# Block kernel on one core: maxima sent from SyncE, the attention division on GpSimd, and a reordered closing part

## The chip, the cores and the metric

The kernel runs on 1 core of one Trainium2 chip. The metric is the device time of one execution in microseconds, the median of several runs. The core has TensorE (PE, matmuls and transposes), VectorE (DVE), ScalarE (ACT), GpSimd (POOL) and SyncE (SP, which here issues DMAs only). ACT also issues some DMAs; while it issues one, it starts no computation.

## The reference

A pre-norm transformer block on 16 sequences of 256 tokens, width 256, all in float32. Attention has 16 heads of width 16; a key more than 16 places ahead of the query is masked. The feed-forward part has 1024 units and weights that are interpolated from control points.

```python
scores = jnp.einsum('bihd,bjhd->bhij', q, k) * scale
mask = idx[None, :] - idx[:, None] > WINDOW // 2
scores = jnp.where(mask[None, None, :, :], -jnp.inf, scores)
attn = jax.nn.softmax(scores, axis=-1)
out = jnp.einsum('bhij,bjhd->bihd', attn, v).reshape(b, s, d)
...
x = x + _L0_attn_ref(_layernorm(x, axis=-1), wq, wk, wv, wo)
x = x + _L0_ffn_ref(_layernorm(x, axis=-1), gate_cp, up_cp, down_cp)
# _L0_ffn_ref: (silu(h @ gate_w.T) * (h @ up_w.T)) @ down_w.T
```

## The kernel before

Every engine runs its instructions in the order in which the program lists them (`InOrder`), so the order of the calls is the schedule. The main loop goes over steps s = 0 to 16 and works on several sequences at once: `nb = s-1` is having its score maxima found, `tb = s-2` its exponentials taken, `ob = s-3` its attention divided and projected, `gb = s-4` its gate and up products made, and `db = s-5` its down sums. The projections for sequence s+3 are spread over the step in places called gaps (`project(s, gap)`). From step 13 on (`LATE`) there is no such sequence, so these steps have less TensorE work. After step 16 a closing part, written out by hand, finishes the last sequences; `last` is 15.

A step has six score visits: `inner(nb, tb, g)` for the groups g = 0 to 3 and `outer(nb, tb, 0)` and `(…, 1)`, in the order inner 0, inner 1, outer 0, inner 2, inner 3, outer 1. A visit writes raw scores for `nb` and scores less their maxima for `tb` into two PSUM tiles (`tiles`, named scores in the profile). Then `read` empties them: ACT takes exponentials (`e`) of one tile while DVE finds maxima (`z`, `mx`) in the other, and then they change over; POOL masks the exponentials (affine selects). The next visit's matmuls wait until both tiles have been read. What TensorE does in between are fillers: `project`, `down` sums (eight units for each half of a sequence, two recorded matmuls a unit), `gate_up`, `values`, `project_o`, and transposes.

The maxima reach the scores by way of a row of the key tile: `turn_max` transposes the maxima of half the groups (pm), ACT copies them (mxT), and two DMAs that ACT issues write them into row 31 of `qks`. Half 0 serves the visits inner 0, inner 1 and outer 0 of the next step, half 1 the other three. In the loop before, `turn_max(nb, 1)` is the last thing in a step.

The sums of the exponentials make a round trip through DRAM. `gather` sends them (den) and the heads' outputs (ac) from `au` on SP at the end of a step. In the next step `invert` takes the reciprocal on DVE in the middle of inner 0 (after it for s < 4), and SP then issues, in this order: two DMAs of feed-forward inputs (`feed`), `send_inverse` (rd), two more of `feed`, and `spread_inverse`, four DMAs (rb) that wait for rd to land. `divide` multiplies ac by rb, and `project_o` (py) needs the product. `stats_f`, `norm_f`, `turn_f` and `features` make the feed-forward input from it. All results of `project_o`, `values`, `turn_max`, `turn_f`, `features` and most `down` sums share two PSUM buffers (`ps_m`).

In the closing part the order before is: inner 0 and 1 together, four SP items as above, `down(12, 0)`, outer 0, `divide(14)`, half a down sum, `gate_up(13, 0)`, `project_o(14)`, `values(15, 0)`, then inner 2 and 3, outer 1, and the feed-forward part of sequences 13 to 15. No maxima are left to be found there, so DVE has no part in its visits.

Of the kernel before, what the change touches and what calls it, by code (L numbers as in the profile page):

```python
# [141 lines left out]
def block_kernel(  # L142
# [354 lines left out]
    def inner(nb, tb, *groups, between=None):  # L497

        has_n, has_t = 0 <= nb < B, 0 <= tb < B
        qn, qt = qks[nb % NQK], qks[tb % NQK]  # L500
        places = [(g, S * gi, S * gi if len(groups) > 1 else S) for gi, g in enumerate(groups)]
        for g, at_t, at_n in places:
            if has_n:
                if g == 0:
                    mxs[nb] = sb.tile([P, 2, H], F32, tag="mx", name=f"mx{nb}")
                scores(qn, True, g, P, at_n, P + HB + LOOK)
            if has_t:
                scores(qt, False, g, HB, at_t + HB - LOOK, S - HB + LOOK)
            if has_n:
                scores(qn, True, g, P + HB, at_n, S)  # L510
            if has_t:
                scores(qt, False, g, 0, at_t, S)

        def exponentials(pr):
            for g, at, _ in places:
                e = sb8.tile([P, 2, S], F32, tag="e0", name=f"e0{tb}_{g}_{pr}")
                act.activation(e, tiles[pr][:, :, at : at + S], AF.Exp, scale=HD**-0.5)

                pool.affine_select(
                    out=e[:, :, 0:M0], in_=e[:, :, 0:M0],  # L520
                    compare_op=ALU.is_ge, fill=0.0, base=LOOK,
                    pattern=[[0, 2], [1, M0]], channel_multiplier=-1,
                )
# [44 lines left out]
    def turn_max(b, half):  # L568
        mx = mxs[b] if half == 0 else mxs.pop(b)
        pm = ps_m.tile([H // 2, S], F32, tag="m", name=f"pm{b}_{half}")  # L570
        for c in range(2):
            pe.transpose(
                pm[:, c * P : (c + 1) * P], mx[:, c, H // 2 * half : H // 2 * (half + 1)], ident
            )
        mxT = sb.tile([H // 2, S], F32, tag="mxT", name=f"mxT{b}_{half}")
        act.copy(mxT, pm)
        for i in range(2):
            act.dma_start(qks[b % NQK][31:P:32, 0, 2 * half + i, :], mxT[4 * i : 4 * i + 4, :])


    def values(b, g2):
# [32 lines left out]
    def invert(b):  # L614
        den = recs.pop(b)
        rec = sb.tile([4 * H, 64], F32, tag="rec", name=f"rec{b}")
        dve.reciprocal(rec, den)
        recs[b] = rec
# [45 lines left out]
                )  # L664
        recs[b] = pr

    def divide(b):
        dve.tensor_tensor(aos[b], aos[b], recs.pop(b), ALU.mult)


    def project_o(b):
        py = ps_m.tile([P, 2, DIM], F32, tag="m", name=f"py{b}")
        ao = aos.pop(b)
        for c in range(2):
            for kc in range(2):
                pe.matmul(
                    py[:, c, :],
                    lhsT=ao[:, kc, c * P : (c + 1) * P],
                    rhs=w_in["o"][:, kc, :],
                    start=(kc == 0),  # L680
                    stop=(kc == 1),
                )
        dve.tensor_tensor(xs[b], xs[b], py, ALU.add)

    def stats_f(b):
        norm_stats(b, "f")
# [91 lines left out]
    def do(stage, b, *args):  # L778
        if 0 <= b < B:
            stage(b, *args)  # L780
# [56 lines left out]
    def project(s, gap):  # L837
        for stage, *what in early.get((s, gap), ()):
            stage(*what)
        pb = s + AHEAD  # L840
        for stage, b, at, *what in (
            (stats_a, pb + 1, 1),
            (scale_xT, pb, 1),
            (first_part, pb, "a"),
            (send_factors, pb + 1, "b"),
            (second_part, pb, 4),
            (load_xT, pb + 1, 4),
            (spread, pb, 4),
            (spread_factors, pb + 1, 5),
            (project_v, pb, 6),  # L850
        ):
            if at == gap and b >= RAW:
                do(stage, b, *what)
# [10 lines left out]
    for s in range(B + 1):  # L864
        nb, tb, ob, gb, db = s - 1, s - 2, s - 3, s - 4, s - 5
        late = s >= LATE

        if s < 4:
            inner(nb, tb, 0)
            project(s, 1)  # L870
            do(invert, ob)
        else:
            inner(nb, tb, 0, between=(lambda: invert(ob)) if ob < B else None)
        do(feed, ob - 1, (0,))
        do(send_inverse, ob)
        do(feed, ob - 1, (1,))
        do(spread_inverse, ob)
        if s >= 4:
            project(s, 1)
        do(down, db, 0, ALL[0:4] if late else ALL[0:6], ALL, fb[:, 0, 0:DIM])  # L880
        inner(nb, tb, 1)
        if late:
            down(db, 0, ALL[4:8])
        else:
            do(down, db, 0, ALL[6:8])
            do(down, db, 1, ALL[0:4])
        project(s, 2)
        outer(nb, tb, 0)
        do(divide, ob)
        project(s, 3)  # L890
        if late:
            down(db, 1, ALL[0:3], ALL[0:4])
        else:
            do(down, db, 1, ALL[4:8])
            do(send_out, db)
        do(gate_up, gb, 0)
        project(s, "a")
        if late:
            down(db, 1, ALL[3:4], ALL[0:4])
        do(project_o, ob)  # L900
        project(s, "b")
        inner(nb, tb, 2)
        if s <= 1:
            project(s, 4)
        do(stats_f, ob)
        if s > 1:
            project(s, 4)
        if late:
            do(turn_max, nb, 0)
            down(db, 1, ALL[4:6], ALL[4:6], fb[:, 1, 0:DIM])  # L910
        inner(nb, tb, 3)
        do(norm_f, ob)
        project(s, 5)
        if not late:
            do(turn_max, nb, 0)
        do(values, tb, 0)
# [24 lines left out]
    down(last - 3, 0, ALL)  # L941
    outer(-1, last, 0)
    divide(last - 1)
    down(last - 3, 1, FIRST, FIRST)
    gate_up(last - 2, 0)
    project_o(last - 1)
    values(last, 0)
    stats_f(last - 1)
    inner(-1, last, 2, 3)
    norm_f(last - 1)  # L950
    down(last - 3, 1, SECOND, SECOND)
    send_out(last - 3)
    turn_f(last - 1)
    send_samples(last - 1)
    outer(-1, last, 1)
    down(last - 2, 0, FIRST, FIRST)
    gate_up(last - 2, 1)
    values(last, 1)
    aos[last] = sb1.tile([P, 2, S], F32, tag="ac", name=f"ac{last}")
    invert_last(last)  # L960
    features(last - 1)
    feed(last - 1)
    invert_rows(last)
    down(last - 2, 0, SECOND, SECOND, tiles[0][:, 1, 0:DIM])
    down(last - 2, 1, ALL[0:2], ALL, tiles[0][:, 0, 0:DIM])
    spread_last(last)
    divide(last)
    down(last - 2, 1, ALL[2:4])
    project_o(last)
    stats_f(last)  # L970
    norm_f(last)
    down(last - 2, 1, ALL[4:8])
    send_out(last - 2)
    gate_up(last - 1, 0)
# [5 lines left out]
    down(last - 1, 0, FIRST + SECOND, FIRST + SECOND)  # L980
    gate_up(last, 0)
    down(last - 1, 1, FIRST, FIRST)
    gate_up(last, 1, (tiles[0], tiles[1]))
    down(last - 1, 1, SECOND, SECOND)
    send_out(last - 1)
    order = FIRST + SECOND
    halves = [fb[:, n, 0:P] for n in range(2)]
# [53 lines left out]
```

## Time and profile before

| | |
|---|---|
| three runs | 537.41, 531.87, 530.50 us; median 531.87 |
| the profiled execution's own time | 533.38 us |
| its span, first to last instruction | 531.3 us |
| busy: PE / DVE / ACT / POOL | 492.3 / 354.1 / 230.9 / 154.7 us |
| PE busy, 150 to 350 us | 197 of 200 us |
| PE busy, 375 to 450 us | 66.7 of 75 us |
| PE busy, 475 us to the end | 47.2 of 56.3 us |
| granted TensorE clock, mean | 0.99 |

The profile is one execution. A line of the timeline gives an instruction's start, its length, its engine and what it writes and reads; "idle before" is time in which the engine did nothing, with what ended it. "q" behind an engine's name means its sequencer, which issues DMAs. PE records of matmuls overlap, so the start of the next group tells more than the length of one. Steps 5 to 12 start 29 us after one another, steps 13 to 16 27.2 us.

### The profile page before, as it was taken

What the parts mean: (1) busy time and instruction counts of PE and PEld (TensorE: products, weight loads), DVE (VectorE), ACT (ScalarE), POOL (GpSimd) and SP (SyncE); (2) the same over time, 40 slices, a digit from 0 to 9 for tenths busy, and PEclk for the clock granted to TensorE, in tenths of its full rate; (3) what the DMA queues carried; (4) which work ended last, traced back from release to release, by engine and by line L of the source; (5) the groups of instructions that cost most, each with busy time, mean ns of one, the idle gap of its engine ahead of it and who ended that gap; (6) DMA issues with size and microseconds to landing.
All of it is one profiled execution on the core that took longest, in us unless ns stands there. A gap on an engine that the chain in (4) does not pass through costs nothing. (4 is left out here: it accounts for less than half of the span.)

```text
span 531.3 us, 18475 instructions
## 1 busy us (share of the span) xinstructions
PE 492.3 (93%) x7491; PEld 349.9 (66%) x7491; DVE 354.1 (67%) x1468; ACT 230.9 (43%) x434; POOL 154.7 (29%) x282
## 2 busy tenths in 40 slices
PE   8998969899999999999999999999898989899987
PEld 7666655457767677776777776766565656566656
DVE  4786356576777667676867677676878686835463
ACT  1236343545363635445454636354444444453130
POOL 6338541222323232323223232322222221222000
PEclk9999998989999999999999999999999999998999
DMA  3541833315243434434252423323040404041231
GB/s 118 145 97 41 259 90 92 110 35 155 64 131 102 111 104 113 124 83 143 61 155 72 133 81 94 122 62 106 15 132 3 144 4 147 3 144 40 81 101 41
DMA packets 53241, 51.26 MB, mean 96 GB/s; under 512 B 6354, under 2 KB 52100, under 8 KB 53156
## 3 DMA queue, kind: packets, MB, share of 16 engines
q1 hardware_dynamic: 46772, 44.24, 28.6%
q10 hardware_dynamic: 6384, 5.84, 3.6%
q8 instruction: 59, 0.97, 0.8%
q14 instruction: 26, 0.21, 0.1%
HBM read 24.12 MB, written 12.84 MB: 70 GB/s over the span
## 5 line engine op out<-in xcount | busy, mean ns | idle before, releaser
L136 DVE CUSTOM_DVE_ANT_0 z<-scores,mask 128x144 bf16<-128x144 f32 (+1 forms) x512 | 156.4, 362 | 85.4 <-issue 38.5
L136 ACT ACTIVATE e<-scores 128x512 f32<-128x512 f32 (+1 forms) x192 | 114.9, 615 | 140.0 <-PE scores L136 74.4
L136 POOL TENSOR_SCALAR_AFFINE_SELECT e<-e 128x224 f32<-128x224 f32 (+1 forms) x192 | 92.4, 487 | 278.3 <-ACT e L136 275.7
L136 PE MATMUL scores<-qk 31*64 31x208 f32 (+7 forms) x4096 | 105.7, 318 | 19.7 <-ACT e L136 11.1
L136 PEld LDWEIGHTS scores<-qk 32*64 32x64 f32 (+1 forms) x4096 | 70.2, 131 | 52.2 <-ACT e L136 36.8
L136 PE MATMUL pd<-downT,inter 128*128 128x256 f32 x216 | 53.8, 390 | 0.5 <-DVE inter L136 0.5
L136 PE MATMUL po<-e,v 128*32 128x256 f32 (+1 forms) x1024 | 51.4, 339 | 1.4 <-POOL e L136 0.9
L136 PEld LDWEIGHTS po<-e,v 128*32 128x32 f32 x1024 | 30.1, 111 | 23.9 <-issue 9.5
L136 DVE SCALAR_TENSOR_TENSOR th<-th,scores 128x512 f32<-128x512 f32 x34 | 23.4, 687 | 33.6 <-ACT th L136 33.6
L136 PEld LDWEIGHTS pd<-downT,inter 128*128 128x128 f32 x216 | 39.2, 189 | 9.7 <-issue 2.5
L136 DVE DVE_READ_ACCUMULATOR2_ANT mx<- 128x1 f32 x512 | 42.5, 83 | 0.0
L136 PE MATMUL fb<-downT,inter 128*128 128x256 f32 x168 | 41.9, 391 | 0.0
L136 PE MATMUL fb<-feat,gate_w 32*64 32x256 f32 x480 | 40.5, 395 | 0.8 <-DMA feat<-via 0.7
L136 ACT ACTIVATE th<-scores 128x512 f32<-128x512 f32 x34 | 20.1, 597 | 45.3 <-PE scores L136 45.3
L136 PE MATMUL scores<-feat,gate_w 32*64 32x256 f32 x544 | 36.7, 394 | 1.3 <-ACT e L136 1.2
L136 PEld LDWEIGHTS fb<-downT,inter 128*128 128x128 f32 x168 | 30.1, 189 | 11.0 <-DVE inter L136 3.9
L136 PE MATMUL py<-wo,ac 128*128 128x256 f32 x128 | 31.7, 392 | 5.0 <-issue 2.6
L136 ACT COPY au<-po 128x512 f32<-128x512 f32 x32 | 18.7, 586 | 30.6 <-PE po L136 15.5
L136 PE MATMUL pk<-xT,wk 128*128 128x256 f32 x128 | 31.7, 390 | 0.0
L136 PE MATMUL pq<-xT,wq 128*128 128x256 f32 x120 | 30.4, 397 | 0.5 <-ACT xT L136 0.5
L136 PEld LDWEIGHTS py<-wo,ac 128*128 128x128 f32 x128 | 24.5, 194 | 9.5 <-issue 3.2
L136 PE MATMUL pv<-wv,xT 128*128 128x256 f32 x120 | 30.0, 390 | 0.0
(94 smaller groups left out, 615.4 us busy)
## 6 DMA issues: line engine op xcount, KB each, us to landing
qk<-qkc SPq DMA_DIRECT2D x31, 256.0 KB
feat<-via SPq DMA_DIRECT2D x62, 128.0 KB
x<-x SPq DMA_DIRECT2D x16, 256.0 KB
ac<-au SPq DMA_DIRECT2D x32, 128.0 KB
via<-x2T SPq DMA_DIRECT2D x16, 256.0 KB
via<-x2T ACTq DMA_DIRECT2D x16, 256.0 KB
rb<-rd SPq DMA_DIRECT2D x60, 64.0 KB
out<-x SPq DMA_DIRECT2D x15, 256.0 KB
```

Source lines behind the costliest of these rows:

```text
L136: return self.tc.keep_in_program_order(fn(*args, **kwargs))
```

## The change

- `turn_max` no longer sends. A new `send_max` does it. From step 4 on SP issues the sends: half 0 in the second half of the step, half 1 in the following step behind `spread_inverse`. For s < 4 ACT still does it. In steps 13 to 16 `turn_max` of half 1 also moves into the following step, behind inner 0.
- `divide` runs on POOL from step 4 to 16 and is listed ahead of outer 0 (before: on DVE, behind it). In step 3 it stays on DVE, but behind inner 2, with `project_o` and `stats_f` behind inner 3 and `norm_f` behind outer 1.
- The addition of `project_o`'s result becomes a call of its own, `add_o`; in steps 13 to 16 it is behind inner 2.
- In steps 13 to 16 the eight units of `down(db, 0)` stand as 4, 3 and 1 (the last behind outer 0) in place of 4 and 4, and in the shared PSUM buffers.
- The closing part has all its visits first, with only `down(12, …)` between them, and the rest in a new order behind them.

```diff
@@ turn_max
         act.copy(mxT, pm)
+        mxTs[b, half] = mxT
+
+    mxTs = {}
+
+    def send_max(b, half, queue=sp):
+        mxT = mxTs.pop((b, half))
         for i in range(2):
-            act.dma_start(qks[b % NQK][31:P:32, 0, 2 * half + i, :], mxT[4 * i : 4 * i + 4, :])
+            queue.dma_start(qks[b % NQK][31:P:32, 0, 2 * half + i, :], mxT[4 * i : 4 * i + 4, :])
...
-    def divide(b):
-        dve.tensor_tensor(aos[b], aos[b], recs.pop(b), ALU.mult)
+    def divide(b, engine=dve):
+        engine.tensor_tensor(aos[b], aos[b], recs.pop(b), ALU.mult)
...
-        dve.tensor_tensor(xs[b], xs[b], py, ALU.add)
+        pys[b] = py
+
+    pys = {}
+
+    def add_o(b):
+        dve.tensor_tensor(xs[b], xs[b], pys.pop(b), ALU.add)
@@ main loop
-            inner(nb, tb, 0, between=(lambda: invert(ob)) if ob < B else None)
+            inner(nb, tb, 0, between=lambda: invert(ob))
+        if late:
+            turn_max(tb, 1)
         do(feed, ob - 1, (0,))
         do(send_inverse, ob)
         do(feed, ob - 1, (1,))
         do(spread_inverse, ob)
-        if s >= 4:
+        if s > 4:
+            send_max(tb, 1)
+        if not first:
             project(s, 1)
-        do(down, db, 0, ALL[0:4] if late else ALL[0:6], ALL, fb[:, 0, 0:DIM])
+        if late:
+            down(db, 0, ALL[0:4])
+        else:
+            do(down, db, 0, ALL[0:6], ALL, fb[:, 0, 0:DIM])
         inner(nb, tb, 1)
         if late:
-            down(db, 0, ALL[4:8])
+            down(db, 0, ALL[4:7])
...
         project(s, 2)
+        if not first:
+            divide(ob, pool)
         outer(nb, tb, 0)
-        do(divide, ob)
         project(s, 3)
         if late:
+            down(db, 0, ALL[7:8])
             down(db, 1, ALL[0:3], ALL[0:4])
...
-        do(project_o, ob)
+        if not first:
+            project_o(ob)
+        if not (first or late):
+            add_o(ob)
         project(s, "b")
         inner(nb, tb, 2)
         if s <= 1:
             project(s, 4)
-        do(stats_f, ob)
+        if first:
+            do(divide, ob)
+        elif late:
+            add_o(ob)
+        if not first:
+            stats_f(ob)
         if s > 1:
             project(s, 4)
         if late:
-            do(turn_max, nb, 0)
+            turn_max(nb, 0)
+            send_max(nb, 0)
             down(db, 1, ALL[4:6], ALL[4:6], fb[:, 1, 0:DIM])
         inner(nb, tb, 3)
-        do(norm_f, ob)
+        if first:
+            do(project_o, ob)
+            do(add_o, ob)
+            do(stats_f, ob)
+        else:
+            norm_f(ob)
         project(s, 5)
         if not late:
             do(turn_max, nb, 0)
+            if first:
+                do(send_max, nb, 0, act)
         do(values, tb, 0)
         if s:
             do(load_x, s + 2 + AHEAD)
+        if not (first or late):
+            send_max(nb, 0)
         outer(nb, tb, 1)
+        if first:
+            do(norm_f, ob)
         project(s, 6)
...
-        do(turn_max, nb, 1)
+        if s + 1 < LATE:
+            do(turn_max, nb, 1)
+        if first:
+            do(send_max, nb, 1, act)
         project(s, 7)
@@ closing part, the new order whole
     inner(-1, last, 0, 1)
+    turn_max(last, 1)
     invert(last - 1)
     feed(last - 2, (0,))
     send_inverse(last - 1)
     feed(last - 2, (1,))
     spread_inverse(last - 1)
+    send_max(last, 1)
+    down(last - 3, 0, ALL[0:5])
     outer(-1, last, 0)
+    down(last - 3, 0, ALL[5:8])
+    inner(-1, last, 2, 3)
+    down(last - 3, 1, ALL)
+    send_out(last - 3)
+    outer(-1, last, 1)
     divide(last - 1)
+    values(last, 0)
     gate_up(last - 2, 0)
+    values(last, 1)
+    aos[last] = qks[(last - 1) % NQK][:, 0, 0:2, :]
+    invert_last(last)
     project_o(last - 1)
+    add_o(last - 1)
     stats_f(last - 1)
+    gate_up(last - 2, 1, (tiles[0], tiles[1]))
+    invert_rows(last)
+    down(last - 2, 0, FIRST, FIRST + SECOND, fb[:, 0, 0:DIM])
+    spread_last(last)
     norm_f(last - 1)
+    divide(last)
+    down(last - 2, 1, FIRST[0:2], FIRST + SECOND, fb[:, 1, 0:DIM])
     turn_f(last - 1)
     send_samples(last - 1)
+    project_o(last)
     features(last - 1)
     feed(last - 1)
+    add_o(last)
     stats_f(last)
     norm_f(last)
+    down(last - 2, 1, FIRST[2:4], FIRST + SECOND)
+    down(last - 2, 0, SECOND, FIRST + SECOND)
+    down(last - 2, 1, SECOND, FIRST + SECOND)
     send_out(last - 2)
     turn_f(last)
     send_samples(last)
+    gate_up(last - 1, 0)
     features(last)
     gate_up(last - 1, 1, (tiles[0], tiles[1]))
     feed(last, (0, 1), sp, act)
+    down(last - 1, 0, FIRST, FIRST + SECOND)
+    down(last - 1, 1, FIRST, FIRST + SECOND)
     gate_up(last, 0)
+    down(last - 1, 0, SECOND, FIRST + SECOND)
     gate_up(last, 1, (tiles[0], tiles[1]))
+    down(last - 1, 1, SECOND, FIRST + SECOND)
     send_out(last - 1)
```

More of the change, by code (lines that the diff above doesn't have):

```diff
@@ L866, in block_kernel @@
         late = s >= LATE
-        if s < 4:
+        first = s < 4
+        if first:
             inner(nb, tb, 0)
@@ L929, in block_kernel @@
         do(features, ob)
-        do(turn_max, nb, 1)
+        if s + 1 < LATE:
+            do(turn_max, nb, 1)
+        if first:
+            do(send_max, nb, 1, act)
         project(s, 7)
@@ L940, in block_kernel @@
     spread_inverse(last - 1)
-    down(last - 3, 0, ALL)
+    send_max(last, 1)
+    down(last - 3, 0, ALL[0:5])
     outer(-1, last, 0)
+    down(last - 3, 0, ALL[5:8])
[3 more added lines that the diff above has]
+    outer(-1, last, 1)
     divide(last - 1)
-    down(last - 3, 1, FIRST, FIRST)
+    values(last, 0)
     gate_up(last - 2, 0)
+    values(last, 1)
+    aos[last] = qks[(last - 1) % NQK][:, 0, 0:2, :]
+    invert_last(last)
     project_o(last - 1)
-    values(last, 0)
+    add_o(last - 1)
     stats_f(last - 1)
-    inner(-1, last, 2, 3)
+    gate_up(last - 2, 1, (tiles[0], tiles[1]))
+    invert_rows(last)
+    down(last - 2, 0, FIRST, FIRST + SECOND, fb[:, 0, 0:DIM])
+    spread_last(last)
     norm_f(last - 1)
-    down(last - 3, 1, SECOND, SECOND)
-    send_out(last - 3)
+    divide(last)
+    down(last - 2, 1, FIRST[0:2], FIRST + SECOND, fb[:, 1, 0:DIM])
     turn_f(last - 1)
     send_samples(last - 1)
[L955 to L960, printed above, removed]
+    project_o(last)
     features(last - 1)
     feed(last - 1)
[L963 to L969, printed above, removed]
+    add_o(last)
     stats_f(last)
     norm_f(last)
-    down(last - 2, 1, ALL[4:8])
+    down(last - 2, 1, FIRST[2:4], FIRST + SECOND)
+    down(last - 2, 0, SECOND, FIRST + SECOND)
+    down(last - 2, 1, SECOND, FIRST + SECOND)
     send_out(last - 2)
-    gate_up(last - 1, 0)
     turn_f(last)
     send_samples(last)
+    gate_up(last - 1, 0)
     features(last)
@@ L979, in block_kernel @@
     feed(last, (0, 1), sp, act)
-    down(last - 1, 0, FIRST + SECOND, FIRST + SECOND)
+    down(last - 1, 0, FIRST, FIRST + SECOND)
+    down(last - 1, 1, FIRST, FIRST + SECOND)
     gate_up(last, 0)
-    down(last - 1, 1, FIRST, FIRST)
+    down(last - 1, 0, SECOND, FIRST + SECOND)
     gate_up(last, 1, (tiles[0], tiles[1]))
-    down(last - 1, 1, SECOND, SECOND)
+    down(last - 1, 1, SECOND, FIRST + SECOND)
     send_out(last - 1)
```

## The prediction

> **What bounds the kernel now.** I read the busy shares first. TensorE (PE) is busy 93% of the span, and between 150 and 350 us it is busy 197 of 200 us. So time can only be won where PE waits, and nothing can be won from making another engine shorter. The list of PE's waits says for whom.
>
> ```profile
> PE 492.3 (93%) x7491; PEld 349.9 (66%) x7491; DVE 354.1 (67%) x1468; ACT 230.9 (43%) x434; POOL 154.7 (29%) x282
> ...
> PE scores L136 <- ACT e L136: 12.3, 17, 1.2
> PE scores L136 <- DVE mx L136: 7.4, 13, 1.2
> PE py L136 <- issue: 2.6, 1, 2.6
> PE py L136 <- DVE ac L136: 2.5, 1, 2.5
> ```
>
> Most waits are score visits whose tiles have not been read yet; two long ones are `project_o` (py) waiting for the division. Next I read the timeline of one visit, inner 0 of step 14, and the same place in step 8.
>
> ```profile
> 387.18 1.04 PE L136 MATMUL scores<-qk 31*64 31x208 f32 x32
> 388.18 0.36 ACT L136 COPY mxT<-pm 8x256 f32<-8x256 f32 x1 [0.53 <-ACT x2T L136]
> 388.57 1.08 ACTq L136 DMA_DIRECT2D qk<-mxT  x2
> 389.77 1.09 ACT L136 ACTIVATE e<-scores 128x512 f32<-128x512 f32 x2 [1.23 <-DVE rec L136]
> 390.40 0.42 DVE L136 CUSTOM_DVE_ANT_0 z<-scores,mask 128x256 bf16<-128x256 f32 x1 [0.79 <-ACT e L136]
> 391.32 1.04 PE L136 MATMUL scores<-qk 31*64 31x208 f32 x32 [1.18 <-DVE mx L136]
> ...
> 248.31 1.05 PE L136 MATMUL scores<-qk 31*64 31x208 f32 x32 [0.31 <-DVE mx L136]
> ```
>
> The scores are there at 388.2, but ACT copies the maxima and issues their two DMAs first, so its exponentials start 1.5 us late, DVE's second maxima follow them, and PE waits 1.18 us. In step 8 two more down units hide all but 0.31. Last I looked at the two long waits and at the granted clock behind them, in stretches of 3.4 us.
>
> ```profile
> 78.95 0.72 DVE L136 TENSOR_TENSOR ac<-ac,rb 128x512 f32<-128x512 f32 x1 [2.42 <-DMA rb<-rd]
> 79.77 2.38 PE L136 MATMUL py<-wo,ac 128*128 128x256 f32 x8 [2.55 <-issue]
> ...
> 77.77:81.19 3.42, 1.42 (x7) 1.29 (x8) 1.98 (x4) 0.00 (x0) 2.06 (x3) 1.00 0.06 18
> 81.19:84.60 3.41, 3.41 (x37) 1.74 (x36) 0.89 (x2) 0.56 (x2) 0.00 (x0) 0.50 0.06 13
> ...
> 477.13:480.55 3.42, 1.04 (x5) 0.94 (x6) 1.75 (x4) 1.09 (x2) 0.00 (x0) 1.00 0.10 32
> 480.55:483.96 3.41, 3.41 (x25) 1.87 (x27) 3.31 (x7) 0.00 (x0) 0.00 (x0) 0.50 0.00 0
> ```
>
> The second number is PE's busy time, the third from the right the clock. After a stretch in which PE idled 2.0 or 2.4 us the clock is 0.50 for the next 3.4 us: a long wait costs itself and then up to 1.7 us more. (A third such stretch follows 1.55 us of idling at 105 to 108.)
>
> **Step 3: −3.6 us.** Division and `project_o` move behind inner 2 and inner 3. PE then goes from the sum for v (end 77.2) through pf (0.3) straight to inner 2 at 77.5, not 82.3. DVE divides behind that visit's maxima, near 80.1, when rb (landed 78.9) is there. I followed PE from there: the spline 2.0, inner 3 at 80.7 (1.0), py 1.9, spline 2.0, pm 0.3, `values` 1.5, outer 1 at 87.4 (1.1), the v projection 1.9, to 90.4. The transpose ptf now waits: DVE has outer 1's maxima until 90.4 and `norm_f` 0.8 behind them, so 91.2. `values` of the second half begin at 91.75, before at 95.33: 3.6 gained. Bounds: −1.9 if ptf waits longer, −4.3 if the whole wait and half clock go (2.55 and 1.7).
>
> **Steps 5 to 12, ACT's sends gone: −2.4 us.** Inner 0's exponentials start 1.1 us sooner; both tiles are read 3.45 us after the visit's start (scores to first maxima 1.3, two maxima 0.7, reciprocal 0.55, two maxima 0.75, 0.15 to PE). PE's own work there is 1.0 and six units of 0.49, 3.9. So the wait of 0.29 to 0.32 goes eight times: 2.4. SP gets four issues of 0.5 us a step. The first two stand behind rb, in step 7 at 222.8, eight us ahead of inner 2 at 231.1; the other two behind the x load at 238.4, 5.5 ahead of inner 0. Behind them on SP are the projection's transfers and the next samples, which wait for ACT anyway (231.5, 241.3). The division on POOL takes 1.27 us (the row below), from about 3.2 us behind the last rb issue: in step 7 226.0 to 227.3, with py at 229.2. What waits behind it on POOL are outer 0's selects, needed by `values` at 235.3. Cover is 1.9 us; without it each 0.3 turns into a loss. Bounds: 0 and −2.4.
>
> ```profile
> L136 POOL TENSOR_TENSOR xT<-xT,fa 128x512 f32<-128x512 f32 x9 | 11.4, 1271 | 0.0
> ...
> L136 DVE TENSOR_TENSOR ac<-ac,rb 128x512 f32<-128x512 f32 x15 | 12.3, 819 | 9.6 <-DMA rb<-rd 9.2 <-issue 0.3
> ```
>
> **Steps 13 to 16: +0.7 us.** Inner 0 gets shorter by 0.7 and by the 0.3 of the transposes that leave the place ahead of it, so PE comes to py 1.0 us sooner. But rb doesn't: SP's chain from the den send (0.6 + 1.3 + 1.4 + rd 0.6 + 1.5 + rb 2.3 and the landing) has no part that moves. In step 16 rb lands at 452.0, POOL's 1.27 makes it 453.3, PE is ready at 452.3 and waits 1.1; py began at 453.28 before. Of step 13 to 16 I get +0.4, −0.1, +0.5, +0.3 at py, from the DVE divisions' starts 370.8, 397.6, 425.4 and 452.2: 1.1 in all. From py to outer 1 DVE sets the pace, before from 453.53 with no gap (four products 2.65, two additions, eight maxima, statistics, to 461.55). The same items stand behind py now, a little denser (8.3 in place of 8.4 us, 0.4 in four steps). The unit moved behind outer 0 fills PE's wait for `tiles[1]` there, and leaves 0.5 of wait behind inner 1. Bounds: −2.4 with the DVE row's 0.69 for the division, +4 if the new waits bring two half-clock stretches. The price lies next to the POOL row, since this has the same shape.
>
> **Closing part: +4.4 us.** PE starts at 468.3: inner 0 and 1 1.05, pm 0.3, five units 2.4, outer 0 0.65, three units 1.5, done at 474.3. Inner 2 and 3 then need the second half of the maxima, and their DMAs now stand on SP behind rb:
>
> ```profile
> 471.66 0.56 SPq L136 DMA_DIRECT2D rd<-rec  x1
> 472.32 1.23 SPq L136 DMA_DIRECT2D feat<-via  x2
> 473.80 2.28 SPq L136 DMA_DIRECT2D rb<-rd  x4
> ```
>
> They are issued at 476.1 and 476.65. No row shows their landing. From below it is the den send's 1.9 us (468.12 to the reciprocal at 470.03), from above the last rb's 3.2 (475.57 to the division at 478.77): 478.55 to 479.85. I take 478.8, near den, the other small one. **PE waits 4.5 us**, more than the 2.46 it waited for py, which is gone. Behind it: both visits and eight units 5.0, outer 1 0.65, `values` 1.5, gate and up 1.05, `values` 1.5, `project_o` 1.9, gate and up 1.05, four units 1.95, to 493.45. DVE has meanwhile products 2.65 from 487.8, addition and statistics 1.95, products 2.65, the last reciprocal 1.0: 496.05, so pr waits 2.65. Then pr 1.1, two units 1.0, ptf 0.45, `project_o` 1.9, pn 1.0: 501.5; ten units and ptf, 506.8. The samples of 14 take from pn's end copy 0.65, landing 2.2 (508.68 to 510.87), issue 0.65, landing 2.8 (511.56 to 514.4): 507.85, a wait of 1.05. Those of 15 come 6.5 behind their pn (507.95 to 514.44 before): 516.35. The rest is 14.0 us of work as before and 0.2, so the last matmul ends at 530.5, before at 528.45: +2.1. The first wait brings a half-clock stretch (1.5, part of it falls into the wait), the second in about half of all cases (0.8). Bounds: 0 and +8.5.
>
> The Trainium skill (TensorE: Matmul & The Clock Gate, Part 1: The HAM clock gate) lets the clock fall only after a window of about 3.4 us that is idle. Here stretches that were idle for 1.55 to 2.4 us of 3.4 were followed by half clock, so the rows decide; by the page the wait of 2.65 would cost no clock and the sum would be 0.8 us lower.
>
> **Sum.** −3.6 − 2.4 + 0.7 + 4.4 = −0.9 on the profiled execution's 533.4 us: 532.5. That execution is 1.5 us above the median of the three runs, so I forecast **531.0 us**.
>
> **Rivals.**
> *The closing part loses nothing* (the maxima land while PE still has work, or the chain behind catches up): −5.3, 528.1, on the median's scale 526.6. For it: nearly all of PE's work there is the same, and 2.46 and a half-clock stretch go. Against: SP's issue times. 0.25.
> *The wait for the maxima in the closing part outweighs everything* (slower than before). Landing at 479.85 adds 1.05, both half-clock stretches whole 3.4, and the samples' chains 1.5 where they were still covered: +8.0. 533.4 − 5.3 + 8.0 = 536.1, 534.6 on the median's scale. It decides once that part loses over 5.3. For it: nothing else can be run during the wait. 0.22.
> *The change only moves the waits.* rb lands later at step 3 (−1), the 0.3 a step return as waits for POOL (0), steps 13 to 16 lose 1.5, the closing part 4.4: 538.3, or 536.8. Against: 1.9 us of cover. 0.08.
> My forecast, 528 to 533.5, has 0.45.
>
> **Range and chances.** 525 to 538 takes in all cases and leaves out only the sums of all bounds at one end (522.8 and 542.5 on the median's scale). A measurement of this kernel tells about 2%, 10.6 us, from no change. Faster by over that needs 521.2, below every case: 0.03. Slower, 542.5, needs waits in all four places: 0.05. Within: 0.92.
>
> **What would show it.** Right: no wait at py in step 3 and full clock behind it; no wait of 0.3 between inner 0 and inner 1 in steps 5 to 12; py in steps 13 to 16 released by POOL's ac after a wait near 1 us; a wait of 4 to 5 us at the closing part's inner 2, ended by the DMA of qk, then a stretch at 0.50. It is wrong if that wait is under 2 us, or if py waits in steps 5 to 12.

## The result, and the profile after

The changed kernel takes 535.71 us (median of 20 runs, 530.92 to 540.35), the kernel before 532.35 us (20 runs, 528.14 to 537.41). The ratio is 1.0064, with a 95% interval of 1.0042 to 1.0087: 3.4 us slower. The forecast was 531.0 us, a gain of 0.9; the time lies within the range, but the change goes the other way, as the second rival had it ("the wait for the maxima in the closing part outweighs everything", 534.6). The interval leaves out 1, so the loss is small but clear. Runs over 1.5% above the fastest of their kernel are left out of the ratios and of the means below. The profiled execution of after took 535.79 us with a span of 534.1.

The first two views are those with which the prediction began, the busy line and the list of PE's waits (total, times, longest, in us).

```profile
PE 491.5 (92%) x7491; PEld 351.6 (66%) x7491; DVE 341.1 (64%) x1452; ACT 231.7 (43%) x434; POOL 168.2 (32%) x295
...
PE scores L136 <- ACT e L136: 14.4, 17, 1.9
PE py L136 <- POOL ac L136: 6.2, 5, 2.9
PE scores L136 <- DMA qk<-mxT: 5.1, 1, 5.1
PE pr L136 <- DVE rec L136: 2.8, 1, 2.8
PE fb L136 <- DMA feat<-via: 1.7, 2, 1.0
...
PE scores L136 <- DVE mx L136: 1.1, 2, 0.8
```

PE does the same work as before; the waits are others. Visits that waited for DVE's maxima have gone from 7.4 to 1.1 us, and both waits of 2.5 us at py are gone. In their place py waits 6.2 us for the division on GpSimd, one score visit 5.1 us for a DMA, and pr 2.8 us for a reciprocal. The groups show the division's price, which the prediction took from another row of the same shape (1271 ns):

```profile
L136 POOL TENSOR_TENSOR ac<-ac,rb 128x512 f32<-128x512 f32 x13 | 16.5, 1270 | 54.2 <-DMA rb<-rd 54.2
```

Next the timeline of step 14, from inner 0 to py, with the engines named in the lines.

```profile
381.36 0.60 ACT L136 ACTIVATE e<-scores 128x512 f32<-128x512 f32 x1 [0.54 <-PE scores L136]
382.22 0.60 ACT L136 ACTIVATE e<-scores 128x512 f32<-128x512 f32 x1 [0.27 <-DVE mx L136]
382.72 0.34 ACT L136 COPY mxT<-pm 8x256 f32<-8x256 f32 x1
...
383.31 0.55 SPq L136 DMA_DIRECT2D rd<-rec  x1
...
383.34 1.04 PE L136 MATMUL scores<-qk 31*64 31x208 f32 x32
...
386.25 1.14 PE L136 MATMUL scores<-qk 31*64 31x80 f32 x64 [0.37 <-ACT e L136]
...
387.43 2.23 SPq L136 DMA_DIRECT2D rb<-rd  x4
...
392.71 1.27 POOL L136 TENSOR_TENSOR ac<-ac,rb 128x512 f32<-128x512 f32 x1 [6.13 <-DMA rb<-rd]
...
394.04 3.34 PE L136 MATMUL py<-wo,ac 128*128 128x256 f32 x8 [2.90 <-POOL ac L136]
```

The upper part is what the change is for, and it works: ACT takes its exponentials at once, copies the maxima behind them, and inner 1 at 383.34 has a wait of 0.13 where it had 1.18. The lower part is what it costs here. SP issues rd at 383.31, but rb only at 387.43, 4.12 us later (2.09 in this step before). PE has nothing left to do at 391.14, and waits 2.90 for POOL. The eight matmuls of py then take 3.34 us: the clock is at half. The stretches of 3.4 us show it, and those behind the two waits of the closing part. The columns are the stretch, then the busy times of PE, PEld, DVE, ACT and POOL, the granted clock, and DMA.

```profile
390.90:394.31 3.41, 0.51 (x3) 0.28 (x2) 2.99 (x5) 0.78 (x2) 1.60 (x2) 1.00 0.07 23
394.52:397.91 3.39, 3.39 (x23) 2.23 (x30) 0.00 (x0) 0.00 (x0) 0.65 (x2) 0.50 0.00 0
473.00:476.40 3.40, 0.27 (x12) 0.30 (x20) 0.00 (x0) 0.00 (x0) 0.00 (x0) 1.00 0.17 58
476.41:479.80 3.39, 3.39 (x37) 2.27 (x22) 0.00 (x0) 1.82 (x4) 0.94 (x3) 0.51 0.02 5
493.50:496.90 3.40, 1.99 (x12) 1.78 (x13) 2.51 (x5) 0.00 (x0) 0.00 (x0) 1.00 0.01 2
496.93:500.30 3.37, 3.37 (x11) 2.85 (x10) 0.00 (x0) 0.59 (x1) 0.00 (x0) 0.50 0.22 76
```

Last the closing part, SP's issues and PE's two waits.

```profile
470.65 2.26 SPq L136 DMA_DIRECT2D rb<-rd  x4
473.00 1.12 SPq L136 DMA_DIRECT2D qk<-mxT  x2
...
476.13 1.79 PE L136 MATMUL scores<-qk 32*64 32x208 f32 x32 [5.07 <-DMA qk<-mxT]
...
494.91 1.12 PE L136 MATMUL pr<-rec,heads 32*128 32x128 f32 x8 [2.79 <-DVE rec L136]
```

Cut at ACT's second copy of the heads' outputs (au) in each step, the two profiled executions compare as follows (us):

| part | before | after | difference | predicted |
|---|---|---|---|---|
| to the end of step 2 | 63.3 | 62.5 | −0.7 | 0 |
| step 3 | 33.7 | 31.9 | −1.8 | −3.6 |
| step 4 | 30.1 | 28.6 | −1.4 | 0 |
| steps 5 to 12 | 231.8 | 229.5 | −2.2 | −2.4 |
| steps 13 to 16 | 108.8 | 111.8 | +3.1 (step 14 alone +3.6) | +0.7 |
| closing part | 63.8 | 69.7 | +5.9 | +4.4 |

### The profile page after: what moved, and what is told of

It reads as the page before. It is cut to its first block, busy times and chain, and to the rows that moved or that the text cites. A ratio compares the mean times of both kernels' runs of the same rounds, so it can differ in the third digit from the quotient of the medians.

```text
span 534.1 us, 18479 instructions
## 1 busy us (share of the span) xinstructions
PE 491.5 (92%) x7491; PEld 351.6 (66%) x7491; DVE 341.1 (64%) x1452; ACT 231.7 (43%) x434; POOL 168.2 (32%) x295
## 4 chain that ended last, share of the span: by engine, by line
PE 55%; DMA 10%; DVE 6%; SPq 4%; issue 3%; POOL 2%; ACT 2%; POOLq 0%; ACTq 0%
PE scores L136 14%; PE fb L136 9%; PE pd L136 7%; PE po L136 6%; PE py L136 5%; SPq L136 4%; DMA rb<-rd 3%; PE pv L136 3%; PE pk L136 3%; DMA rd<-rec 3%; PE pq L136 3%; DMA via<-x2T 2%; PE pn L136 2%; DVE z L136 2%; POOL ac L136 1%
## 5 line engine op out<-in xcount | busy, mean ns | idle before, releaser
L136 DVE CUSTOM_DVE_ANT_0 z<-scores,mask 128x144 bf16<-128x144 f32 (+1 forms) x512 | 154.7, 360 | 84.6 <-issue 37.7
L136 ACT ACTIVATE e<-scores 128x512 f32<-128x512 f32 (+1 forms) x192 | 116.8, 615 | 162.8 <-PE scores L136 89.5
L136 POOL TENSOR_SCALAR_AFFINE_SELECT e<-e 128x224 f32<-128x224 f32 (+1 forms) x192 | 90.3, 477 | 211.2 <-ACT e L136 210.1
L136 PE MATMUL pd<-downT,inter 128*128 128x256 f32 x248 | 61.9, 393 | 0.0
L136 PEld LDWEIGHTS pd<-downT,inter 128*128 128x128 f32 x248 | 45.9, 193 | 10.2 <-issue 3.6
L136 PE MATMUL fb<-feat,gate_w 32*64 32x256 f32 x464 | 36.9, 388 | 1.7 <-DMA feat<-via 1.7
L136 PE MATMUL fb<-downT,inter 128*128 128x256 f32 x136 | 34.0, 391 | 0.0
L136 POOL TENSOR_TENSOR ac<-ac,rb 128x512 f32<-128x512 f32 x13 | 16.5, 1270 | 54.2 <-DMA rb<-rd 54.2
L136 PEld LDWEIGHTS py<-wo,ac 128*128 128x128 f32 x120 | 22.9, 196 | 11.8 <-POOL ac L136 8.2
L136 PEld LDWEIGHTS fb<-downT,inter 128*128 128x128 f32 x136 | 24.4, 189 | 8.8 <-DVE inter L136 3.1
```

Of the source, the lines that this page charges most:

```text
L136: return self.tc.keep_in_program_order(fn(*args, **kwargs))
```

## The experiments

Each kernel was run in turn with the kernel before on the same chip, and ratios are to that kernel. "Late steps" are steps 13 to 16. A to D ran on one chip, E to H, then I, K and L, then M to P on three others, so two kernels of different groups are compared by way of their ratios.

The record has the granted clock of each run, so the time that half clock cost can be worked out as (1 − clock) x span. The column "clock" is its mean over a kernel's runs, and "rest" is the mean time less that, both in us. For the kernel before they are 2.4 to 3.4 and 528.6 to 528.7 on the four chips, for the change 6.7 and 528.7. By this estimate the two kernels are even apart from the clock, and the whole loss of the change is half clock. The rest still holds about 0.2 to 0.9 us of uncertainty (one standard error).

| kernel | ratio to before | 95% interval | clock | rest |
|---|---|---|---|---|
| A: the changed loop, closing part of before | 0.9933 | 0.9903 to 0.9962 | 3.1 | 524.5 |
| B: loop of before, changed closing part | 1.0170 | 1.0135 to 1.0205 | 7.5 | 532.3 |
| C: change, closing maxima sent by ACT | 0.9907 | 0.9882 to 0.9932 | 2.9 | 523.0 |
| D: change, late division on DVE | 1.0022 | 0.9995 to 1.0049 | 6.0 | 526.2 |
| E: C with the reciprocals' rows earlier | 0.9892 | 0.9849 to 0.9935 | 2.3 | 522.9 |
| F: before with step 3's moves alone | 0.9945 | 0.9917 to 0.9973 | 2.3 | 526.4 |
| G: before with SP's sends alone | 0.9932 | 0.9899 to 0.9966 | 4.0 | 523.5 |
| H: D and E together | 0.9881 | 0.9845 to 0.9918 | 2.0 | 522.6 |
| I: F and G, closing part of E | 0.9856 | 0.9815 to 0.9897 | 4.0 | 519.8 |
| K: F and G, closing part of before | 0.9799 | 0.9770 to 0.9829 | 1.1 | 520.3 |
| L: I with GpSimd dividing in steps 4 to 12 | 0.9806 | 0.9775 to 0.9837 | 2.7 | 519.1 |
| M: L with the late respread of `down` | 0.9830 | 0.9794 to 0.9866 | 2.0 | 520.2 |
| N: L with GpSimd dividing in late steps too | 0.9855 | 0.9820 to 0.9890 | 3.1 | 520.4 |
| O: L with the late addition | 0.9831 | 0.9799 to 0.9863 | 2.2 | 520.1 |
| P: L with the closing part of before | 0.9841 | 0.9807 to 0.9875 | 2.2 | 520.4 |

### Loop or closing part: A and B

A takes the closing part back, B takes only the closing part over:

```diff
@@ A, against the change: the order of before, with its maxima sent by ACT
-    inner(-1, last, 0, 1)
     turn_max(last, 1)
+    send_max(last, 1, act)
+    inner(-1, last, 0, 1)
...
     spread_inverse(last - 1)
-    send_max(last, 1)
...
@@ B, against the kernel before: the order of the change
     inner(-1, last, 0, 1)
+    turn_max(last, 1)
...
     spread_inverse(last - 1)
...
+    send_max(last, 1)
...
```

> The changed main loop with the closing part of before (maxima of sequence 15 sent by ACT ahead of it). Theory: the loss lies in the closing part (5.9 us in the two profiles) and the loop gains about 3, so this is faster than before by 1 to 5 us, ratio 0.990 to 0.998, and the stretch from the last copy of au in step 16 to the end is 63 to 65 us. Rival: steps 13 to 16, where py now waits for the division on GpSimd, lose what the rest of the loop wins; then the ratio is 1.000 to 1.006.

> The loop of before with the changed closing part alone. Theory: slower than before by 4.5 to 6.5 us, ratio 1.008 to 1.012, with a wait of 4.5 to 5.5 us for the DMA of the maxima ahead of the visits of groups 2 and 3 and one of 2.5 to 3 us ahead of pr. Rival: the closing part is even and the loss arises in steps 13 to 16; then the ratio is 0.997 to 1.003.

A measured 527.71 us, 3.5 under the kernel before on that chip; B measured 540.16, 9 above it. So the loop of the change is a gain, somewhat smaller than the −5.3 of the prediction, and the closing part loses 7 us (the change against A) to 9 us (B), not 4.4. Less the clock the part loses 4.2 us by the change against A (528.7 and 524.5) and 3.7 by B (532.3 and 528.6); the other half of the loss is half clock. B's profile shows why it can be more than in the profile of after: the same waits of 4.64 and 2.79 us, but each with a half-clock stretch of twice the length. Four stretches of B around the first wait:

```profile
467.29:470.70 3.41, 3.41 (x46) 2.55 (x44) 0.12 (x1) 2.51 (x6) 1.72 (x5) 1.00 0.75 216
470.70:474.10 3.40, 0.30 (x2) 0.00 (x0) 0.42 (x1) 0.16 (x1) 0.92 (x2) 1.00 0.36 124
474.10:477.52 3.42, 1.88 (x32) 1.17 (x32) 0.00 (x0) 0.00 (x0) 0.00 (x0) 0.50 0.06 19
477.52:480.92 3.40, 3.40 (x12) 2.71 (x9) 0.00 (x0) 2.06 (x4) 1.53 (x4) 0.50 0.02 5
```

The clock falls at 474.10, in the middle of the wait (471.00 to 475.64). The first stretch at half clock idles 1.54 us itself, and the next one is at half clock too. In after the wait ends 0.27 us ahead of the stretch's end, and only one stretch follows. The falls of the clock lie on a raster: those of after, at 70.26, 394.53, 476.44 and 496.93, are 95.0, 24.0 and 6.0 times 3.413 us apart. So where the wait lies on this raster seems to decide over 1.7 us each time.

### What in the closing part: C and E

C lets ACT send the second half of the maxima at once; nothing else of the change differs. E also calls `invert_rows`, which pr needs, one item earlier:

```diff
@@ C, against the change
     turn_max(last, 1)
+    send_max(last, 1, act)
...
     spread_inverse(last - 1)
-    send_max(last, 1)
@@ E, against C
+    invert_rows(last)
     gate_up(last - 2, 1, (tiles[0], tiles[1]))
-    invert_rows(last)
```

> The changed kernel, but in the closing part ACT sends the maxima of sequence 15 as soon as it has copied them, not SyncE behind the four rb transfers. Theory: the wait of 5 us falls below 0.5, no stretch of half clock follows it, and the kernel is 4 to 6 us faster than the changed one: ratio to before 0.994 to 1.000. The wait of 2.8 ahead of pr stays, since VectorE's chain there starts from the same PE work. Rival: PE waits there for something else as well (the exponentials, the division of 14), and under 2 us are won: ratio 1.003 to 1.007.

> The changed kernel with the closing part's maxima sent by ACT at once and the reciprocal of sequence 15 (invert_rows) ahead of the second gate_up of sequence 13. Theory: VectorE's four products there were what made pr wait 2.8 us; with the reciprocal ahead of them pr waits under 0.5, no stretch of half clock follows, and the kernel is 3 to 6 us faster than with the ACT send alone: ratio to before 0.979 to 0.986. Rival: the next link, the samples of 14 and 15 by way of DRAM, takes the time back as a longer wait at the gate_up calls; then under 2 us are won, ratio 0.987 to 0.991.

C measured 525.88 us, 0.9907: one queue changed for two small DMAs turns a loss of 0.6% into a gain of 0.9%, 8 us, more than was expected (0.994 to 1.000). Of these 8 us the clock makes up 3.8. Its timeline has ACT's issues and inner 2 without a wait:

```profile
464.04 1.07 ACTq L136 DMA_DIRECT2D qk<-mxT  x2
...
466.18 1.39 PE L136 MATMUL scores<-qk 32*64 32x208 f32 x32
```

and of the three new waits only two are left in its list:

```profile
PE py L136 <- POOL ac L136: 3.9, 4, 1.6
PE pr L136 <- DVE rec L136: 2.8, 1, 2.8
```

E measured 525.37 us, 0.9892, which isn't told apart from C and lies where the rival had it (522.9 and 523.0 less the clock). Its profile has no wait at pr and a closing part of 60.8 us (C: 64.7, the kernel before: 63.8), but E's profiled execution lost 3.7 us in step 14 as the change's did: a landing of rd of 4.17 us.

### The division on GpSimd: D and H

```diff
@@ D, against the change (H: the same against E)
-        if not first:
+        if not (first or late):
             divide(ob, pool)
         outer(nb, tb, 0)
+        if late:
+            divide(ob)
```

> The changed kernel with the division on VectorE behind outer 0 in steps 13 to 16 only. Theory: py waits for the transfer rb more than for the engine, so only the difference of the two durations comes back, 0.6 us a step: 1 to 2.5 us faster than the changed kernel, ratio to before 1.002 to 1.005. Rival: GpSimd's place in those steps is what costs (its masks wait behind the division, half-clock stretches follow), and 4 us come back: ratio 0.997 to 1.000.

> As x5_rows_first, with the division of steps 13 to 16 on VectorE behind outer 0. Theory: the 2 us that this brought to the changed kernel come here too: 1 to 2.5 us faster than x5_rows_first, ratio to before 0.976 to 0.983. Rival: without the long waits behind it there is nothing left that this shortens, and both are even.

D measured 1.0022, 2.2 us under the change, as the theory had it, though the two intervals overlap. H measured 0.9881, even with E's 0.9892: there the division's place is not worth a measurable amount. The two left open what the late steps lose, and to what.

### Single parts of the loop: F and G

```diff
@@ F, against the kernel before
-        do(divide, ob)
+        if s > 3:
+            do(divide, ob)
...
+        else:    # step 3: behind inner 2; project_o, stats_f behind inner 3, norm_f behind outer 1
+            do(divide, ob)
@@ G, against the kernel before
-            act.dma_start(qks[b % NQK][31:P:32, 0, 2 * half + i, :], mxT[4 * i : 4 * i + 4, :])
+            queue.dma_start(...)    # SP from step 4 on, in the places of the change
```

> The kernel before with step 3's moves alone (division behind inner 2, project_o and stats behind inner 3, norm_f behind outer 1). Theory: the wait of 2.55 us and the half clock behind it go, a wait of about 0.9 at ptf comes: 1.5 to 3.6 us faster than before, ratio 0.993 to 0.997. Rival: the wait only moves; ratio 0.999 to 1.001.

> The kernel before with the sends of the maxima on SyncE from step 4 on, as in the change (in steps 13 to 16 with the transposes of half 1 behind inner 0), but the division on VectorE in its old place, the down sums as before, and the closing part of before. Theory: 0.3 us a step in steps 5 to 12 and, since py then waits for rb and not for GpSimd, 0.3 to 0.6 a step in steps 13 to 16: 3 to 5 us faster, ratio 0.990 to 0.995. Rival: SyncE's four more issues a step delay rb, and the gain is under 1.5 us: 0.997 to 1.000.

F measured 528.24 us (0.9945, −3 us) and G 527.56 (0.9932, −3.6 us). Step 3's term of −3.6 and the sends' −2.4 are both there; the sends are worth more. Together 6.6 us, but A, which has both and the late steps' other edits besides, has only 3.5. So these other edits seem to lose about 3 us.

### Putting the parts together: I, K and L

```diff
@@ I and K: the edits of F and G together; closing part of E (I) or of before (K)
@@ L, against I
+        if s > 3 and not late:
+            do(divide, ob, pool)
         outer(nb, tb, 0)
-        if s > 3:
+        if late:
             do(divide, ob)
```

> The sends and step 3's moves of the change without its division on GpSimd (DVE divides everywhere), and the changed closing part with its maxima sent by ACT and the reciprocals' rows ahead of gate_up(13, 1). Theory (the parts add up): the sends gave 3.6 us, step 3 gave 3.0, the mended closing part some 2 beyond the old one: 8 to 9 us under the kernel before, a ratio of 0.983 to 0.986. In the profile steps 13 to 16 take 105 to 109 us. Rival (the parts share their gain: what one wins the next wait takes): no better than the 0.988 to 0.989 of the two kernels with a division on GpSimd.

> The same loop with the closing part of before (its maxima sent by ACT): differs from the changed loop with the old closing part in the division, and in the order of some late fillers. Theory (the division on GpSimd costs time in the late steps): 3.6 + 3.0 = 6.6 us under the kernel before, 0.987 to 0.989, against 0.9933 with the changed loop. Rival (the division's place doesn't matter, the parts don't add up): 0.992 to 0.994.

> As the first kernel of this call, but GpSimd divides in steps 4 to 12, ahead of outer 0; DVE still does in steps 13 to 16. Theory (in steps 5 to 12 the division on GpSimd is covered by 1.9 us): equal to the first kernel within 0.002, steps 5 to 12 together 228 to 230 us in both. Rival (a slow landing of rd in steps 9 and 12 makes PE wait for GpSimd there): 1 to 3 us slower than the first kernel, with a wait at py released by POOL's ac in step 9 or 12.

They measured 524.44, 522.11 and 521.18 us; 0.9856, 0.9799 and 0.9806. I lies where "the parts add up" had it; K, expected at 0.987 to 0.989, is better than that: it is 2.0% under the kernel before (9.9 us by the medians), and so beats both kernels, as L does. The clock has a share in that: K's profile has no half-clock stretch ahead of its end, where before has three and F and G two each. Less the clock, F gains 2.3, G 5.2 and K 8.4 us, so the parts do add up. Against A, which has the same closing part, K's ratio is 0.0134 lower, 7 us (4.2 less the clock); the division on GpSimd and the late edits that K leaves out cost about that. L was expected within 0.002 of I and came out 0.005 below it, which the intervals do not tell apart. It shows that the division on GpSimd does next to no harm in steps 5 to 12: they take 228.3 us in L and 228.5 in I, and py does not wait there, though rd lands late in steps 9 and 12 in both (3.46 to 3.97 us); the 1.9 us of cover hold. (The cover is thin: in step 9 py waits 0.4 us in D, M and N, 1.1 in H.) I's profiled execution took 105.1 us for the late steps, with rd landing within 2.3 us in all of them; K's and L's each had a late landing in step 14, L's also a wait of 1.77 us at py in step 13 with half clock behind it, and they took 107.1 and 108.9.

### Which late edit: M, N, O, and the closing part again: P

```diff
@@ M, against L: late steps
-        do(down, db, 0, ALL[0:4] if late else ALL[0:6], ALL, fb[:, 0, 0:DIM])
+        if late:
+            down(db, 0, ALL[0:4])
...
-            down(db, 0, ALL[4:8])
+            down(db, 0, ALL[4:7])
...
+            down(db, 0, ALL[7:8])
@@ N, against L
-        if s > 3 and not late:
+        if s > 3:
             do(divide, ob, pool)
@@ O, against L: add_o of the late steps behind inner 2, ahead of stats_f
@@ P, against L: closing part of before
```

> The kernel with GpSimd dividing in steps 4 to 12 and DVE behind (0.9806 of the kernel before), with one part of the change added: in steps 13 to 16 down(db, 0) stands as 4, 3 and 1 units in the shared PSUM buffers, where that kernel has 4 and 4 in a place of their own. Theory (the respread is a loss that the prediction put at zero: PE waits 0.37 ahead of outer 0, and py waits for DVE's addition that empties the shared buffer): 0.4 to 1.0 us for each of four steps, 1.5 to 4 us slower, a ratio of 0.983 to 0.988, with py released by DVE's x. Rival (the unit behind outer 0 fills a wait and costs nothing, as the prediction had it): 0.979 to 0.983.

> The same kernel with the division of steps 13 to 16 on GpSimd too, ahead of outer 0; the down units stay 4 and 4. Theory (POOL's 1.27 us in place of DVE's 0.7 stands right between rb's landing and py): 0.5 us a step, 2 us, and more where a half-clock stretch follows: 0.983 to 0.988, with py released by POOL's ac. Rival (py waits for something else there, so that the division's place doesn't matter): 0.979 to 0.983.

> The same kernel with the addition of project_o's result behind inner 2 in steps 13 to 16, as the change has it. Theory (DVE has other work to do first, and the addition is needed only by the statistics behind it): within 0.002 of 0.9806. Rival (the later addition moves outer 1 and the transposes behind it): 0.3 us or more for each step, 0.983 or more, with a longer wait ahead of outer 1.

> The same kernel with the closing part of before (its maxima sent by ACT). Theory (the mended new order is worth the wait of 2 us for the division and little more): 2 to 3 us slower, 0.984 to 0.987, with a wait at py of 2 us. Rival (what the new order wins, its waits at the samples' transfers give back): equal within 0.002.

They measured 522.64, 523.61, 522.30 and 522.91 us, ratios 0.9830, 0.9855, 0.9831 and 0.9841 against L's 0.9806 on another chip. All lie above it by 1.3 to 2.6 us, and none is told apart from it by its interval; the times alone settle none of the four, and less the clock they don't either (all four lie 1.0 to 1.3 us above L). The profiles do it better: the part of a step behind py repeats to 0.1 us within a kernel. The part ahead of it does not, since it hangs on the landings of rd and rb. From the SP issue of den to py, and from there to the next den (steps 14 to 16 without a late rd):

| kernel | den to py | py to next den | step |
|---|---|---|---|
| before | 12.3 to 12.4 | 14.8 | 27.2 |
| I (sends and step 3 alone) | 11.7 to 12.3 | 14.4 | 26.1 to 26.7 |
| L (the base of M, N and O) | 11.8 | 14.4 to 14.5 | 26.2 to 26.3 |
| M (respread) | 11.8 to 12.0 | 14.45 | 26.3 to 26.4 |
| N (division on GpSimd) | 12.1 to 12.9 | 14.15 | 26.3 to 27.1 |
| O (later addition) | 11.8 to 12.0 | 14.85 | 26.6 to 26.8 |
| the change | 12.2 to 12.5 | 14.9 | 27.1 to 27.4 |

So the sends alone make a late step up to 1.05 us shorter, and the three other edits together give nearly all of it back. The one that costs the same in every step is the later addition, 0.4 us behind py; its expectation went to the rival. The respread costs some 0.1 us a step, the division on GpSimd next to nothing in step 15 and 0.8 in step 16, where rb also landed 0.6 us later than in L. The lists of waits do not name the addition, but the timeline of outer 1 does, here in step 14 of O and then of I.

```profile
397.95 1.14 PE L136 MATMUL scores<-qk 31*64 31x80 f32 x64 [1.17 <-ACT e L136]
```

```profile
397.78 1.14 PE L136 MATMUL scores<-qk 31*64 31x80 f32 x64 [0.45 <-ACT e L136]
```

With the addition behind inner 2, DVE comes to the maxima of inner 3 later (6.82 us behind the start of py in O, 6.37 in I), and PE waits 1.17 in place of 0.45 ahead of outer 1. It does so in all four late steps of O and of the change, and 0.45 in all four of before, I, L, M and N. A wait ahead of inner 3 that shrinks from 0.82 to 0.55 gives part of it back. In N py waits for the division, in M for the addition of the down sum that shares the PSUM buffer; one line each from their lists of waits:

```profile
PE py L136 <- POOL ac L136: 5.6, 5, 2.2
```

```profile
PE py L136 <- DVE x L136: 3.0, 4, 1.6
```

P's profile has the wait at py that was expected (2.52 us), but its rival isn't excluded, and K against I went the other way (0.9799 with the old closing part, 0.9856 with the mended new one). In the profiles the closing part takes 61.4 us in L and 62.3 in I with the new order, 62.4 in P and 61.8 in K with the old one. Less the clock, the new order is ahead in both pairs, by 1.3 and 0.5 us, with uncertainties of 0.7. Once its maxima don't stand behind rb, what it is worth is not clear of the noise here.

## Why the prediction was wrong

**The step that failed is the closing part's term, above all its price for the clock.** Its mechanism came as described: SP's queue sets inner 2 (476.13), then half clock, then pr (2.79 for 2.65) and gate_up(14) (0.95 for 1.05). Too small were the sizes in it. The first wait is 5.07 us, not 4.5: PE was done 1.95 us ahead of the maxima's first issue (1.8 in the working), and inner 2 began 3.13 us behind it (2.7). The first half-clock stretch was put at 1.5 us and the second, at half its chance, at 0.8; both came in full, 1.7 each in after. That makes 1.7 us more than 4.4, and the profile has 1.5 more. In B and D, moreover, both stretches last 6.8 us.

Over all runs nearly the whole miss is the clock, by the estimate with which the experiments begin. The prediction's +4.4 was 2.3 for new half clock and 2.1 for the rest, and the rest counted as gone the 1.7 us that the stretch at 480.55 costs before. So it stood at +3.8 without the clock and at +0.6 for the clock. Measured are 4.2 and 3.7 without it (the change against A, B against before), and 3.6 and 5.1 for it. In the median the part loses 7 to 9 us. The upper bound, +8.5, was about right; the value taken wasn't. The prediction itself had put the point from which the closing part decides at 5.3; with the loop's gain at 3.5 it is lower still.

**Steps 13 to 16** were put at +0.7 and came to +3.1, within the bounds (−2.4 to +4); in this pair of profiles that is a larger miss than the closing part's (2.4 against 1.5 us). From den to py the four steps differ from before by −0.6, +1.9, −0.2 and +0.2 us, 1.3 in all. The sum forecast was 1.1 (+0.4, −0.1, +0.5, +0.3), so it came out by luck. Three steps together gained 0.6, and step 14 lost 1.9: rd landed in 4.12 us there, and with py now exposed to the chain den, rd, rb in every late step, the lateness went straight to PE (2.90). The chain itself, from den to rb's last issue, did not move in step 16 (7.43 before, 7.59 after), as the text had it. In the kernel before it was slower in steps 13 and 15 (7.93 and 8.40), and the forecast took that over. Behind py −0.4 was forecast, and +1.8 came: 1.7 is the half clock behind the wait of step 14. That the same items stand "a little denser" there was right for the sends alone (14.4 in place of 14.8), but the later addition took it back.

**Step 3** was put at −3.6. F measured −3.0; in after the profile shows −1.8, with a wait of 1.89 us for exponentials from 66.9 on, ahead of the moved work, and half clock behind it (0.71 and full clock there in before). The kernels that share this code wait between 0.4 and 2.6 us there. The moved division lies behind inner 2's maxima, as the text had it, at 81.19 for 80.1:

```profile
81.19 0.70 DVE L136 TENSOR_TENSOR ac<-ac,rb 128x512 f32<-128x512 f32 x1
...
82.83 1.35 PE L136 MATMUL py<-wo,ac 128*128 128x256 f32 x5
```

with no wait at py. ptf waits 0.94, as followed.

**Steps 5 to 12** were right: −2.2 for −2.4, no wait between inner 0 and inner 1. One of the signs against it did appear, py waiting 0.91 for POOL in step 9, where rd needed 3.93 us, but it costs less than the eight waits bring.

```profile
253.06 1.99 PE L136 MATMUL py<-wo,ac 128*128 128x256 f32 x8 [0.91 <-POOL ac L136]
```

**Step 4**, put at nothing, has −1.4 in this pair of profiles: the half-clock stretch at 108.5 is missing. It comes and goes with the kernels (there in F, L and N, not in the others), so it is not counted as the change's.

On the clock the prediction's rule held where it was used: both long waits of the closing part and that of step 14 were followed by 0.50. It is no threshold, though. In after, stretches of 3.4 us that idled 1.40 (493.5 to 496.9), 2.90 and 3.09 us were followed by half clock, one that idled 1.98 (469.62 to 473.03) was not. In L one that idled 0.88 (481.82 to 485.23) was.

The Trainium skill (TensorE: Matmul & The Clock Gate, Part 1: The HAM clock gate) asks for an idle window of about 3.4 us. Here half clock followed the wait of 2.79 us at pr, so the measurement decides; the estimate by the page, 0.8 us lower, would have been further off.

## What to carry to other kernels

A small transfer that the next matmul needs must not be put behind larger ones on an in-order queue because that queue "has time": in the middle of the kernel there were 5.5 to 8 us of cover, in the closing part none, and the same edit that gains 3.6 us there lost 8 here, half of it by the clock. When cover is removed from a chain through DRAM, price it by its slowest landing in the trace, not by its usual one, and add the clock's price in whole stretches, one or two, not as a chance of a half. And an edit bundled with a good one should be priced against the good one's own new pace: here three edits of the late steps each looked free beside the old step of 27.2 us and took back the 1.05 us that the sends had won.

## What the runs showed of the hardware

*The raster of the clock.* Half clock came in stretches of 3.41 us or 6.83 us. A second one followed where the first itself idled 1.54 us (B), 0.47 us (D, 491.68 to 495.09) or even 0.20 us (C, 483.39 to 486.80); where PE was busy throughout the first, as in after, the clock was full again behind it. That is no threshold either: in before the stretch from 108.49 idled 0.35 us, and full clock followed.

*Late landings of rd at fixed steps.* A 16 KB DMA of 256-byte pieces was followed by its reader's issue in 1.8 to 2.6 us in most steps and in 2.7 to 3.2 in step 4, but in all kernels with SP's sends in step 9 after 3.3 to 4.0 us, in most of them in step 12, and in 14 or 16 in many. In the DMA records each of these late ones has a 16 KB packet of the queue for instructions in the same stretch. In after, from the issue of rd to that of rb, step 14:

```profile
q1 hardware_dynamic: 701, 0.57, 45.4%
q8 instruction: 1, 0.02, 1.4%
```

and step 15 (2.16 us):

```profile
q1 hardware_dynamic: 417, 0.32, 50.0%
```

Counted over steps 4 to 17 of all seventeen profiles: of 49 landings over 2.8 us, 41 have such a packet between 1 us ahead of rd's issue and the reader's issue; of 189 quicker ones, 17 have. The packet's place differs, too. In the 38 late cases of steps 9 to 16 that have one, it begins 2.0 to 2.5 us ahead of the reader's issue; in the 17 quick ones it begins in the last 0.8 us. In before the packet of step 9 begins 0.09 us ahead of the reader's issue, with SP's sends 1.1 to 1.9 us behind rd's. That the packet delays the transfer is thus likely, but not shown: no kernel was run that moves the packets alone.
